# A message-passing kernel: 60 instead of 52 row-wise tiles, another split of their rows between two queues, earlier first loads, and one result write per group

## The chip, the cores and the metric

The kernel runs on one core of one Trainium2 chip. The time is device microseconds of one execution; what is given for the kernel before is the median of 3 runs, 1981.78 us (1979.75 to 1982.48). The profile was taken of a further execution.

The engines are called TensorE (PE in the profile; PEld is its weight load), VectorE (DVE), ScalarE (ACT), GpSimd (POOL) and SyncE (SP). ScalarE and SyncE also issue DMAs; such an issue occupies the engine's queue of instructions and is shown as ACTq or SPq.

## The reference: what is computed

One layer of a graph network over 6250 nodes of 128 features and 206250 edges, which are sorted by their receiver. Cut to what matters:

```python
w = silu(edge_feats @ rad_W1 + rad_b1) @ rad_W2 + rad_b2      # 32 features an edge
w = w + silu(chi @ sph_W1 + sph_b1) @ sph_W2 + sph_b2         # 32 more
q = (x @ Wq)[receivers]; k = (x @ Wk)[senders]; v = (x @ Wv)[senders]
alpha = (q * w * k).reshape(-1, 8, 16).sum(-1) / 4 * cutoffs[:, None]
out = segment_sum(alpha[..., None] * v, receivers) / 16
x = layernorm(x + out)
```

## The kernel before, in words

**Tiling.** 128 edges are a tile, 4 tiles a quad (512 edges), 4 quads a group. There are 403 quads in 101 groups. The loop (lines 770 to 837) runs over groups and, in each, over four slots; each slot handles one quad in each of several stages, so a slot is the unit of time of the loop. `order` is the list of quads in the order of the slots.

**Before the loop** (lines 289 to 507) the table of k and v of all nodes, `kv_tab`, 1 KB a node, is computed and stored in DRAM. For the first 10 quads the x of the senders is gathered instead (`gather_x`, 40 indirect DMAs), and k and v are computed from it.

**Gathers.** For all later quads GpSimd issues one indirect DMA a tile (`gather`, line 134), which fetches 128 rows of `kv_tab` for 128 senders into `kv` (16 buffers). The gathers of a quad are issued 14 quads ahead, and each waits for a matmul of the slot in which it is issued, so that none runs ahead of TensorE by more than that.

**Row-wise tiles.** One tile in each of `ROW_TILES` = 52 quads is not gathered by GpSimd. Its 128 rows are fetched by 128 plain DMAs of 1 KB, issued one by one: 64 by SyncE and 64 by ScalarE (`load_rows`, line 173). The place of a row in the table is read from `at_i` into a register first; one instruction (line 186) fills the registers of up to `ROW_UNIT` = 32 rows, and it is emitted just ahead of the first of these rows. The 52 quads are spread evenly over slots 27 to 392 (`row_at`, line 141), and the rows of each are issued over the slots since the last such quad's rows, ending 8 slots before they are used: 7 or 8 slots for each, so about 9 rows a slot on each of the two queues. In the code order of a slot they come last (line 837), behind the slot's other work on ScalarE and SyncE.

**A slot's work, by engine.** TensorE: one matmul of the group's bookkeeping (lines 243, 252 or 655), the sums of the messages of the group before (line 614), the first layers of quad i+2 (line 516), the queries at the edges of quad i+1 (line 525) and the second layers of quad i+1 (`weigh`, lines 558 and 563). ScalarE: two silus for quad i+2 (line 546), which wait for TensorE's matmuls of that slot, a copy between them, in some slots a scaling of a result (line 693), and then the rows. VectorE: the product with k for quad i+1 (line 575, which waits for the gather), the scores and the messages of quad i (lines 583 to 602), one-hot tables and, for each group, the moments of the layer norm; every fourth group it also computes the inverse roots for four groups (lines 707 to 715). SyncE: x in slot 0 (`load_x`, line 281), edge features in slot 2 (`load_feats`, line 218), receivers in slot 3 (`load_rel`, line 229), finished results (`write_rows`, line 731) and the rows.

**Order.** All of it is written out by hand; every engine does its instructions in the order of the code.

The first loads: x and features of group 0 are issued while `kv_tab` is computed (lines 418 and 501); those of groups 1 and 2 only at the head of the loop (lines 757 to 762), where they stand behind the stores of `rel_lin` (line 506) and between the loads of `relb`.

Results: four groups become ready together, are scaled in four slots in a row, and each is written at least 3 slots later, at most one a slot, in whichever slot comes.

Of the kernel before, what the change touches and what calls it, by code (L numbers as in the profile page):

```python
# [21 lines left out]
SP = mybir.EngineType.SP  # L22
ACT = mybir.EngineType.Activation
# [22 lines left out]
ROW_BYTES = 2 * D * 4  # L46
XQ = 10
RING = 16
ROW_TILES = 52
ROW_FIRST = 20  # L50
ROW_LAST = 392
ROW_LEAD = 8
ROW_UNIT = 32
ROW_ACT = 64
XU = 4
WRITE_LAG = 3
READY_LAG = 2
# [3 lines left out]
XL = 3  # L61
# [6 lines left out]
def gnn_kernel(ctx, tc, x, src, dst, weight, edges, rad_W1, rad_b1, rad_W2, rad_b2,  # L68
# [104 lines left out]
    def load_rows(i):  # L173

        k = next((k for k in range(ROW_TILES) if i <= row_at[k] - ROW_LEAD), None)
        start = None if k is None else (row_at[k - 1] if k else ROW_FIRST) - ROW_LEAD + 1
        if k is None or i < start:
            return
        q = order[row_at[k]]
        slots = row_at[k] - ROW_LEAD + 1 - start  # L180
        table = kv_tab.bitcast(U8).rearrange("(o n) b -> o (n b)", o=1)

        def rows_by(engine, name, a, b):
            for e in range(a, b, ROW_UNIT):
                m = min(ROW_UNIT, b - e)
                rows = nc.values_load_multi_w_load_instructions(
                    at_i[k:k + 1, e:e + m], engines=(name,), min_val=0,
                    max_val=(N - 1) * ROW_BYTES,
                    skip_runtime_bounds_check_because="senders are nodes")[1]
                for p, r in zip(range(e, e + m), rows):  # L190
                    yield lambda p=p, r=r: signalled(engine.dma_start(
                        row_of[q][p:p + 1, 0, :].bitcast(U8), table[:, ds(r, ROW_BYTES)]))

        def signalled(o):
            tc.no_tile_sem_insts.add(o.ins.name)
            tc.add_to_no_dep_group(f"rows_{q}", o.ins)
            o.then_inc(row_sems[k % ROW_SEMS], 16)
            row_count[k % ROW_SEMS] += 16
            row_done[q] = row_sems[k % ROW_SEMS], row_count[k % ROW_SEMS]

        n = P - ROW_ACT
        if i == start:
            row_of[q] = quad_of("wide", 3, P)[:, :2, :].rearrange("p t d -> p (t d)")[:, None, :]
            rows_left[SP].append(rows_by(nc.sync, SP, 0, n))
            rows_left[ACT].append(rows_by(nc.scalar, ACT, n, P))
        for engine, m in ((SP, n), (ACT, ROW_ACT)):
            a, b = (math.ceil(m * j / slots) for j in (i - start, i - start + 1))
            next_rows(engine, b - a)
# [7 lines left out]
    def load_feats(g, mark=None):  # L216
        feats_of[g] = gp.tile([P, EG // 2], F32, name="feats", bufs=3)
        o = nc.sync.dma_start(feats_of[g], edges[g])
        if mark is not None:
            tc.add_manual_dep(o.ins, mark.ins.name, WAIT, reason="one signal of TensorE a quad")  # L220
# [51 lines left out]
    def load_x(g, mark=None):  # L272

        if g not in r_of:
            n = min(XU, NG - g)
            rows = nc.values_load_multi_w_load_instructions(
                gb_i[:1, g:g + n], engines=(SP,), min_val=0, max_val=(N - P) * D * 4,
                skip_runtime_bounds_check_because="the table is clamped to it")[1]
            r_of.update(zip(range(g, g + n), rows))
        x_of[g] = gp.tile([P, D], F32, name="x", bufs=XL + 4)  # L280
        o = nc.sync.dma_start(x_of[g].bitcast(U8), rows_from(x, r_of[g]))
        if mark is not None:
            tc.add_manual_dep(o.ins, mark.ins.name, WAIT, reason="one signal of TensorE a quad")
# [21 lines left out]
    with tc.tile_pool(name="nodes", bufs=1) as nodes, \  # L305
# [76 lines left out]

        rows_f = nodes.tile([P, ROW_TILES], F32, name="rows_f")

# [93 lines left out]
        for i, (k, n) in enumerate(work):  # L478
            if i + 2 < len(work):
                turn(*work[i + 2])  # L480
            kvs = k_and_v(k, n)
            for o, w in smalls[i:i + 1]:
                nc.scalar.dma_start(o, w)
            if i >= len(chunks):
                kv_of[k[0]] = kvs
                a = (i - len(chunks)) * 5 // 4
                for t in range(a * P + P, min(((i - len(chunks) + 1) * 5 // 4 + 1) * P, NT), P):
                    turn_rel(t)
                for f in beside.get(i, []):
                    f()  # L490
                continue
            store(k, kvs)
            if k + 8 < len(chunks):
                load_nodes(k + 8)
            if k == 4:
                nc.sync.dma_start(src_i, src)
            for f in beside.get(k, []):
                f()
            if i == len(chunks) - 1:
                load_rel(0, gp, 1)  # L500
                load_feats(0)
                nc.sync.dma_start(scale, weight)
        for q in order[XQ:AHEAD]:
            gathers(q)
# [5 lines left out]
    with tc.tile_pool(name="ps", bufs=1, space=PSUM) as pp, tc.tile_pool(name="loop", bufs=1) as lp:  # L510
# [243 lines left out]
            nc.vector.tensor_scalar(general, found, 0.0, None, op0=OP.is_gt)  # L754

        written, ready, ready_at = [], [], []
        load_feats(1)
        load_rel(1, lp, 4)
        load_feats(2)
        load_rel(2, lp, 4)  # L760
        for g in range(1, XL):
            load_x(g)
        silus(order[0], first_layers(order[0]))
        pick(1)
        q_at_edges(order[0])
# [4 lines left out]
        for g in range(NG - 1):  # L770
            for slot, j in enumerate((0, 2, 1, 3)):
                q = g * NQ + j
                i = g * NQ + slot
                turned, past, old = None, mark, marks
                if slot == 0 and g == CHECK + len(checks) + 1:
                    verdict()
                if slot == 0:
                    turned = turn_q(g + 1, pp.tile([P, EQ], F32, name="pq", bufs=2))
                if slot == 1 and 2 <= g:
                    turned = sum_group(g - 2)  # L780
                if slot == 2:
                    turned = make_q(g + 1, pp.tile([P, EQ], F32, name="pq", bufs=2))
                if 1 <= g:
                    for t in ((), (0, 1), (2,), (3,))[slot]:
                        mark = sum_quads(g - 1, t)
                first_layers(order[i + 2])
                mark = q_at_edges(order[i + 1])
                marks = weigh(order[i + 1])

                def copies():  # L790
                    if turned:
                        turned()
                    if 1 <= g and slot == 3:
                        part_sums(g - 1)

                silus(order[i + 2], mark, marks, copies)
                if ready and ready_at[-1] <= i:
                    scaled(*ready.pop(0), i)
                if i + AHEAD < len(order):
                    gathers(order[i + AHEAD], old[-QT:])  # L800
                multiply(order[i + 1], mark)
                messages(q, scores(q, marks=marks), marks=marks)
                if slot == 0:
                    if g + XL < NG:
                        load_x(g + XL, past)
                if slot == 2:
                    if g + 3 < NG:
                        load_feats(g + 3, past)
                if slot == 3 and g + 3 < NG:
                    load_rel(g + 3, lp, 4)  # L810
                if slot == 0 and 1 <= g:
                    one_hots(g)
                if slot == 1:
                    one_hots_T(g + 1)
                    if g + 2 < NG:
                        pick(g + 2)
                if slot == 2 and 1 <= g:
                    place(g - 1)
                write_rows(1, i)
                if slot == (3 if g < NG - 2 else 2):  # L820
                    if 2 <= g:
                        statistics(g - 2)
                if slot == 3:
                    if CHECK <= g < CHECK + len(checks):
                        checks[g - CHECK]()
                if g == NG - 3 and slot in (0, 2):
                    wide_one_hots(order[slot // 2 - 3])
                if g == NG - 2 and slot == 0:
                    wide_one_hots(order[-1])
                    n = nc.values_load(general, min_val=0, max_val=1)  # L830
                    place(g)
                    place(NG - 1)
                if g == NG - 3 and slot in (1, 3):
                    weigh_wide(order[slot // 2 - 3])
                if g == NG - 2 and slot == 1:
                    weigh_wide(order[-1])
                load_rows(i)
# [209 lines left out]
```

## Time and profile before

| | |
|---|---|
| median of 3 runs | 1981.78 us |
| the profiled execution | 1977.56 us |
| its span, first to last instruction | 1975.8 us |
| TensorE busy, share of the span | 90% |
| VectorE | 77% |
| GpSimd | 75% |
| ScalarE | 33% |
| gathers issued by GpSimd | 1520 of `kv_tab`, 40 of x |
| rows issued one by one | 3328 by SyncE, 3328 by ScalarE |
| granted TensorE clock, mean | 0.941 |

How to read it: the busy time of an engine leaves out register, semaphore and DMA-issuing instructions, so ScalarE's 33% and SyncE's absence from the list say nothing of how full their queues are. A group of the profile is a line, an engine, an operation and its tiles, with the count, the busy time in us and the mean of one in ns, and behind the bar the idle time of the engine just before, with what ended it.

### The profile page before, as it was taken

The numbers are of one execution on the slowest core, as the hardware profiler recorded it, in microseconds if no ns is written. First come the engines' busy times: TensorE is split into PE (matmuls) and PEld (weight loads), VectorE is DVE, ScalarE is ACT, GpSimd is POOL, SyncE is SP. The second block draws the span as 40 slices with busy tenths as digits, with TensorE's granted clock in tenths as the row PEclk, the third lists the DMA queues.
The fourth block names the chain that finished last, engine by engine and source line by source line (L and its number), as shares of the span: only waits on it lengthen the run. The fifth ranks groups of instructions, "written<-read, shape, count | busy, mean of one in ns | idle before, by whom it ended". The sixth has DMA issues, their size and how long they took to land. (4 is left out here: it accounts for less than half of the span.)

```text
span 1975.8 us, 57697 instructions
## 1 busy us (share of the span) xinstructions
PE 1781.9 (90%) x16014; PEld 1482.9 (75%) x16014; DVE 1520.3 (77%) x3403; ACT 642.5 (33%) x1362; POOL 1481.0 (75%) x1570
## 2 busy tenths in 40 slices
PE   9799999999998999998989889988988888888998
PEld 8687778777777777777877777777767777777776
DVE  6688788888877777777777777776877877777778
ACT  3233333333233333332323332323323333232334
POOL 7777777777777777777777777777777777777775
PEclk9899999999989989899989999899999999898989
DMA  9455555555555555555555555555545455555543
GB/s 318 144 153 155 158 154 157 149 148 151 159 155 156 149 159 152 147 155 145 157 144 156 155 147 154 149 150 149 157 142 158 143 156 155 145 154 147 155 142 94
DMA packets 152293, 304.92 MB, mean 154 GB/s; under 512 B 39852, under 2 KB 86300, under 8 KB 151964
## 3 DMA queue, kind: packets, MB, share of 16 engines
q0 software_dynamic: 74240, 201.95, 36.4%
q1 hardware_dynamic: 69568, 95.42, 15.1%
q10 hardware_dynamic: 8156, 3.82, 0.9%
q8 instruction: 127, 2.08, 0.4%
q14 instruction: 202, 1.65, 0.3%
HBM read 287.58 MB, written 13.46 MB: 152 GB/s over the span
## 5 line engine op out<-in xcount | busy, mean ns | idle before, releaser
L134 POOL DMA_INDIRECT kv<-kv_tab,src_i x1520 | 1440.9, 948 | 469.1 <-PE pw L563 174.0
L546 ACT ACTIVATE act<-ph,b 128x512 f32<-128x512 f32 x806 | 554.8, 689 | 1275.2 <-PE pq L525 767.4
L563 PE MATMUL pw<-w,act 128*128 128x128 f32 x6448 | 883.1, 294 | 0.0
L563 PEld LDWEIGHTS pw<-w,act 128*128 128x128 f32 x6448 | 803.6, 203 | 96.7 <-issue 79.8
L516 PE MATMUL ph<-feats,w 32*128 32x512 f32 x1612 | 521.8, 670 | 38.3 <-ACT act L546 35.7
L525 PE MATMUL pq<-q,hotT 32*128 32x128 f32 x3224 | 489.3, 293 | 19.1 <-DVE kq L575 18.8
L575 DVE TENSOR_TENSOR kq<-pq,kv 128x512 f32<-128x512 f32 (+1 forms) x403 | 270.6, 671 | 285.4 <-DMA kv<-kv_tab,src_i 123.5
L525 PEld LDWEIGHTS pq<-q,hotT 32*128 32x128 f32 x3224 | 409.9, 195 | 49.8 <-DVE kq L575 47.9
L585 DVE TENSOR_REDUCE side<-kq 128x32 f32<-128x512 f32 x403 | 279.8, 694 | 42.7 <-PE pw L563 1.3
L602 DVE TENSOR_TENSOR msg<-kv,side 128x512 f32<-128x512 f32 (+1 forms) x404 | 270.3, 669 | 44.2 <-DVE side L589 2.4
L583 DVE TENSOR_TENSOR kq<-pw,kq 128x512 f32<-128x512 f32 x403 | 274.0, 680 | 0.0
L516 PEld LDWEIGHTS ph<-feats,w 32*128 32x128 f32 x1612 | 143.3, 190 | 144.4 <-ACT act L546 74.1
L558 PE MATMUL pw<-brow,onesb 3*128 3x512 bf16 x403 | 158.9, 394 | 0.6 <-DVE kq L583 0.6
L614 PE MATMUL po<-msg,hot 128*32 128x128 f32 x3200 | 156.8, 294 | 0.0
L655 PE MATMUL pq<-part,to 128*128 128x128 f32 x200 | 48.7, 328 | 88.8 <-DVE kq L575 88.5
L589 DVE TENSOR_TENSOR side<-side,scale 128x32 f32<-128x32 f32 x400 | 79.8, 200 | 42.6 <-DVE side L585 0.9
L655 PEld LDWEIGHTS pq<-part,to 128*128 128x128 f32 x200 | 32.9, 207 | 100.3 <-DVE kq L575 86.7
L614 PEld LDWEIGHTS po<-msg,hot 128*32 128x32 f32 x3200 | 72.3, 112 | 38.9 <-issue 5.6
L258 DVE TENSOR_TENSOR hotT<-relb,side 128x512 f32<-128x512 bf16 x101 | 68.7, 680 | 0.0
L252 PE MATMUL pq<-wq,xT 128*128 128x128 f32 x200 | 44.3, 305 | 26.5 <-DVE kq L575 26.1
L263 DVE TENSOR_TENSOR hot<-rel,side 128x512 f32<-128x512 f32 x100 | 68.0, 680 | 0.0
L252 PEld LDWEIGHTS pq<-wq,xT 128*128 128x128 f32 x200 | 32.4, 203 | 32.1 <-DVE kq L575 31.4
(121 smaller groups left out, 843.7 us busy)
## 6 DMA issues: line engine op xcount, KB each, us to landing
wide<-kv_tab SPq DMA_DIRECT2D x3328, 1.0 KB
wide<-kv_tab ACTq DMA_DIRECT2D x3328, 1.0 KB
feats<-in_edges SPq DMA_DIRECT2D x101, 512.0 KB
kv<-kv_tab,src_i POOLq DMA_INDIRECT x1520
relb<-rel_lin SPq DMA_DIRECT2D x101, 128.0 KB
x<-in_x SPq DMA_DIRECT2D x101, 64.0 KB
out<-y SPq DMA_DIRECT2D x101, 64.0 KB
kv_tab<-kv SPq DMA_DIRECT2D x12, 512.0 KB
```

The lines of the kernel that those rows point to most:

```text
L134: return nc.gpsimd.indirect_dma_start(out=o, out_offset=None, in_=table, in_offset=bass.IndirectOffsetOnAxis(ap=index, axis=0))
L516: return nc.tensor.matmul(act_of[q, i], w1[r0:r0 + R, :], feats_of[g][r0:r0 + R, c0:c0 + EQ], start=True, stop=True)
L525: o = nc.tensor.matmul(pq_of[q][:, t, :], hotT_of[g][b, t * P:(t + 1) * P], q_of[g][b, :], start=True, stop=True)
L546: o = nc.scalar.activation(act, act_of[q, i], AF.Silu, bias=b1[:, i:i + 1])
L558: nc.tensor.matmul(pw, onesb, brow.rearrange("p t d -> p (t d)"), start=True, stop=False)
L563: o = nc.tensor.matmul(pw[:, t, :], act_of[q, i][:, t * P:(t + 1) * P], w2[:, i, :], start=False, stop=(t == QT - 1 and i == 1))
L575: o = nc.vector.tensor_tensor(kq_of[q][:, u, :], pq_of[q][:, u, :], kv[:, :, :D], op=OP.mult)
L583: nc.vector.tensor_tensor(m, pw_of[q][:, t, :], m, op=OP.mult)
L585: o = nc.vector.tensor_reduce(alpha, m.rearrange("p t (h e) -> p t h e", e=HD), AX.X, OP.add)
L602: o = nc.vector.tensor_tensor(msg_of[q][:, u, :].rearrange("p t (h e) -> p t h e", e=HD), kv[:, :, D:].rearrange("p t (h e) -> p t h e", e ...
L614: o = nc.tensor.matmul(po_of[g][j * W:(j + 1) * W, :], hot_of[g][:, j * QT + t, :], msg_of[g * NQ + j][:, t, :], start=(t == 0), stop=(t = ...
L655: nc.tensor.matmul(ph[:, :D], to[:n, 0, :], part[:n, :], start=True, stop=(g == 0))
```

## The change

- `ROW_TILES` goes from 52 to 60. The row-wise quads stand every 6 slots (48 times) or 7 slots (12 times) instead of every 7 or 8; eight gathers leave GpSimd.
- Of the 128 rows of each such tile ScalarE issues 68 and SyncE 60, instead of 64 each.
- The registers are filled 30 rows at a time on SyncE (two fills a tile, as before) and 23 at a time on ScalarE (23, 23 and 22: three fills a tile instead of two).
- x and features of groups 1 and 2 are issued right behind those of group 0, ahead of the load of `scale` and of the stores of `rel_lin`. The loads of `relb` stay where they were.
- A finished result is written only in slot 1 of a group, so one a group instead of up to one a slot.

```diff
-ROW_TILES = 52
+ROW_TILES = 60
 ROW_FIRST = 20
 ROW_LAST = 392
 ROW_LEAD = 8
-ROW_UNIT = 32
-ROW_ACT = 64
+ROW_ACT = 68
+ROW_UNITS = {SP: 30, ACT: 23}
...
         def rows_by(engine, name, a, b):
-            for e in range(a, b, ROW_UNIT):
-                m = min(ROW_UNIT, b - e)
+            for e in range(a, b, ROW_UNITS[name]):
+                m = min(ROW_UNITS[name], b - e)
...
                 load_rel(0, gp, 1)
                 load_feats(0)
+                for g in range(1, XL):
+                    load_x(g)
+                    load_feats(g)
                 nc.sync.dma_start(scale, weight)
...
         written, ready, ready_at = [], [], []
-        load_feats(1)
         load_rel(1, lp, 4)
-        load_feats(2)
         load_rel(2, lp, 4)
-        for g in range(1, XL):
-            load_x(g)
         silus(order[0], first_layers(order[0]))
...
                     place(g - 1)
-                write_rows(1, i)
+                if slot == 1:
+                    write_rows(1, i)
```

`XL` is 3, so the new loop covers groups 1 and 2.

## The prediction

> **What bounds the kernel now.** I read the page first, then GpSimd's part of the waits, then stretches of the run side by side, then ScalarE's timeline, since its queue is what the change loads.
>
> ```profile
> span 1975.8 us, 57697 instructions
> PE 1781.9 (90%) x16014; PEld 1482.9 (75%) x16014; DVE 1520.3 (77%) x3403; ACT 642.5 (33%) x1362; POOL 1481.0 (75%) x1570
> ...
> L134 POOL DMA_INDIRECT kv<-kv_tab,src_i x1520 | 1440.9, 948 | 469.1 <-PE pw L563 174.0
> ```
> ```profile
> POOL kv L134 <- PE pw L563: 174.0, 558, 3.9
> POOL kv L134 <- issue: 157.1, 513, 0.9
> DVE kq L575 <- DMA kv<-kv_tab,src_i: 123.5, 85, 3.5
> ```
> ```profile
> 1959.55 0.95 POOL L134 DMA_INDIRECT kv<-kv_tab,src_i  x1 [0.31 <-issue]
> 1960.80 0.95 POOL L134 DMA_INDIRECT kv<-kv_tab,src_i  x1 [0.30 <-PE pq L657]
> 1962.06 0.95 POOL L134 DMA_INDIRECT kv<-kv_tab,src_i  x1 [0.31 <-PE po L614]
> ```
>
> GpSimd's 75% is a full queue: a gather takes 0.95 us and 0.30 us pass to the next, whatever the releaser named (174.0 us over 558 times is 0.31 us each). The last gather ends at 1963.0 us, 12.8 us ahead of the end of the span. VectorE's largest wait for data is for a gather, 85 times.
>
> ```profile
> core 0: us, PE busy (x) PEld busy (x) DVE busy (x) ACT busy (x) POOL busy (x), PEclk, DMA share, GB/s
> 84.00:123.50 39.50, 39.50 (x398) 34.03 (x398) 35.47 (x68) 15.26 (x30) 29.87 (x32) 1.00 0.54 162
> 200.00:400.00 200.00, 187.66 (x1812) 157.16 (x1811) 165.58 (x361) 70.25 (x149) 150.79 (x160) 0.98 0.53 152
> 600.00:1800.00 1200.00, 1071.13 (x9643) 889.52 (x9641) 904.48 (x1997) 377.67 (x802) 907.80 (x958) 0.93 0.53 151
> ```
>
> These stretches show two regimes. TensorE has 16014 matmuls for 403 quads, 39.7 a quad. Ahead of the rows (84 to 123.5 us) it is busy throughout: 398 matmuls in 39.5 us, 3.94 us for 39.7. From 200 to 400 us, with rows, 1812 matmuls are 45.6 quads, 4.38 us each: compute is still working off the 14 quads that GpSimd is ahead, and is slower than TensorE alone. From 600 us on, 9643 matmuls are 243 quads, 4.94 us each, and 958 gathers in 1200 us are 1.253 us each: GpSimd sets the pace.
>
> **The change, part by part.**
>
> *Eight gathers fewer.* 8 x 1.253 = 10.0 us off GpSimd's queue. Eight more quads have two of VectorE's products split.
>
> ```profile
> 308.49 0.55 DVE L575 TENSOR_TENSOR kq<-pq,kv 128x384 f32<-128x384 f32 x1
> ...
> 308.96 0.28 DVE L575 TENSOR_TENSOR kq<-pq,wide 128x128 f32<-128x128 f32 x1
> ```
>
> Even if the smaller part were wholly added, that is 16 x 0.28 = 4.5 us, which VectorE (75% busy in the last stretch) hides; I put it at 0.
>
> *The first loads.*
>
> ```profile
> 55.93 2.92 DVE L388 TENSOR_SCALAR rows_f<-src_i 128x1 f32<-128x1 int32 x47
> ...
> 61.44 2.17 SPq L445 DMA_DIRECT2D rel_lin<-relT  x2
> ...
> 67.25 2.05 PE L563 MATMUL pw<-w,act 128*128 128x128 f32 x16
> ...
> 68.77 2.46 SPq L281 DMA_DIRECT2D x<-in_x  x3
> ...
> 76.41 0.77 PE L243 MATMUL pq<-pick,x 128*128 128x128 f32 x2 [7.11 <-DMA x<-in_x]
> ...
> 79.53 3.26 PE L563 MATMUL pw<-w,act 128*128 128x128 f32 x16
> ...
> 82.31 0.95 POOL L134 DMA_INDIRECT kv<-kv_tab,src_i  x1 [3.88 <-PE pw L563]
> ```
>
> TensorE waits 7.11 us for x of group 1, then runs a quad's second layers in 3.26 instead of 2.05 us. GpSimd, which may be 14 quads ahead and no more, waits 3.88 us for these matmuls, 3.6 us more than its usual 0.30. With x issued ahead of the store at 61.44 us instead of behind it both go: compute starts 7.1 + 1.2 = 8.3 us sooner, less eight small VectorE instructions at 2.92 / 47 = 0.06 us, say 7.8 us; GpSimd gains 3.6 us. SyncE's four added issues ahead of `scale` and that store I put at 0: until 61.44 us SyncE waits for ScalarE's copies anyway, and `scale` is first used just ahead of the loop, behind the k and v of ten quads, which hide it. Without that cover its 0.8 MB and the 1.1 MB now ahead of it would delay the loop by some us, of the 7.8 just won.
>
> Were GpSimd to stay the bound, the sum would be -10.0 - 3.6 = -13.6 us.
>
> *ScalarE's queue.* This is the part that decides.
>
> ```profile
> 163.84 0.69 ACT L546 ACTIVATE act<-ph,b 128x512 f32<-128x512 f32 x1 [5.13 <-PE pw L563]
> ...
> 164.66 2.13 ACTq L191 DMA_DIRECT2D wide<-kv_tab  x7
> 166.90 0.69 ACT L546 ACTIVATE act<-ph,b 128x512 f32<-128x512 f32 x1 [1.63 <-PE pw L563]
> ...
> 167.72 2.44 ACTq L191 DMA_DIRECT2D wide<-kv_tab  x7
> 170.26 0.69 ACT L546 ACTIVATE act<-ph,b 128x512 f32<-128x512 f32 x1 [1.93 <-PE pq L525]
> 170.72 0.23 ACTq L191 DMA_DIRECT2D wide<-kv_tab  x1
> ...
> 171.04 5.07 ACTq L191 DMA_DIRECT2D wide<-kv_tab  x8
> 176.21 0.69 ACT L546 ACTIVATE act<-ph,b 128x512 f32<-128x512 f32 x1 [4.51 <-PE pw L563]
> ```
> ```profile
> L191 ACTq DMA_DIRECT2D wide<-kv_tab x3328: 227/228/563, 131.4 to 1884.0; - x196
> ```
> ```profile
> L186 SPq TENSOR_LOAD <-at_i x104: 1866/2177/2488, 120.3 to 1862.8; - x104
> L186 ACTq TENSOR_LOAD <-at_i x104: 2130/2204/2500, 128.9 to 1869.6; - x104
> ```
> ```profile
> L276 SPq TENSOR_LOAD <-gb_i x26: 476/572/650, 24.4 to 1889.6; - x26
> ```
>
> A slot without a register fill lasts 3.06 us (163.84 to 166.90) and has 9 rows. Seven rows span 2.13 us, six pitches and one issue of 0.23, so a pitch is 0.317 us; the run of 2.44 us, with one slow issue, gives 0.368. The median issue of 228 ns is the shortest but 1 ns, so I take 0.320. Without its rows the slot is 3.06 - 9 x 0.317 = 0.21 us. The run of 5.07 us with a fill is longer by 5.07 - (7 x 0.317 + 0.23) = 2.62 us, of which the fill is 2.2. Filling 4 registers takes 0.572 us, 32 take 2.204, so one more costs 0.058 us. A fill of 23 was not run; it lies between these two, and by the line through them the 2.62 become 2.10 us.
>
> Before: 3328 x 0.320 + 104 x 2.62 + 372 slots x 0.21 = 1415 us, 81% of the 1752.6 us from the first row to the last. After: 60 x 68 = 4080 rows x 0.320 = 1306, 180 fills x 2.10 = 378, 372 x 0.21 = 78: 1762 us. GpSimd's pace with 7.8 us of an earlier start leaves 1752.6 - 13.6 + 7.8 = 1747 us. So ScalarE's queue is full before it waits for anyone. In a slot it holds back the silus, by them TensorE, by TensorE all else.
>
> ```profile
> L713 DVE TENSOR_TENSOR h<-rs x75: 159/162/208, 124.5 to 1941.9; 128x4 f32<-128x4 f32 x72, 128x1 f32<-128x1 f32 x3
> ```
> ```profile
> 193.76 0.49 PE L655 MATMUL pq<-part,to 128*128 128x128 f32 x2 [1.97 <-DVE kq L575]
> ...
> 197.18 3.78 PE L563 MATMUL pw<-w,act 128*128 128x128 f32 x16
> ```
>
> It does wait: 75 of these in threes are 25 computations of inverse roots on VectorE, and behind one TensorE stands still for 1.97 us, so the silus come late. A slot without a fill now lasts 11 x 0.32 + 0.21 = 3.73 us, so TensorE's usual 3.94 us costs little; I take 1 us of each of the 25 (none to 2 us): 25 us. The rows then last 1762 + 25 = 1787 us from 131.4 - 7.8 = 123.6 on, to 1910.6, which is 26.6 us later than 1884.0.
>
> *Behind the rows* GpSimd's pace falls away, because compute is late and the data is there.
>
> ```profile
> 1964.11 0.39 PE L558 MATMUL pw<-brow,onesb 3*128 3x512 bf16 x1
> ```
>
> Before, 91.8 us pass from the last row to the end; now some 16 quads at 4.1 us (3.94 and the extra work of the last groups) and the 11.7 us behind the last quad's bias matmul: 77.3 us, 14.5 us less. This gain is also the slack by which ScalarE may be late unpunished.
>
> *One write a group* only moves SyncE's issues, which fit (below): 0.
>
> Sum: +26.6 - 14.5 = +12.1 us on the profiled execution's 1977.56, 1989.7 us; that execution is 4.2 us below the median of 1981.78, so 1994 us.
>
> **A rule against a row.** A fill's price by registers is 0.058 us in the rows above. The Trainium skill, Runtime: NRT & Kernel Launch, section Instruction fetch mechanics, has a register load at about 200 ns a register. By that the 32 would take 6.4 us and the fills' 4080 registers 816 us instead of some 300; the estimate would be 2500 us. The row of 2204 ns contradicts it for loads from on-chip memory, so the row decides.
>
> **The rivals.**
>
> 1. *GpSimd stays the bound* (faster): ScalarE's rows, waits included, fit into 1747 + 14.5 = 1761 us; it decides below that, 26 us under my sum. For it: my waits are a guess, and at 0.317 the rows take 12 us less. Against: nothing then may wait. 1977.56 - 13.6 = 1964.0, as a median 1968. That the change nets nothing is the middle between this and the forecast.
>
> 2. *TensorE's clock falls more often.*
>
> ```profile
> PEclk9899999999989989899989999899999999898989
> ```
>
> The clock of 0.93 from 600 to 1800 us means half speed for 14% of the time, there behind idle time. A slot with a fill lasts 5.8 us against TensorE's 3.94, so some 2 us are idle, 180 times. If a fifth of these end in a halved quad whose 1.2 us nothing hides, that is 36 x 1.2 = 43 us: 2037. Against: in a slot with a fill there is room for it. The Trainium skill, TensorE: Matmul & The Clock Gate, section HAM oscillation, sees the danger in idle gaps above about 3.4 us; by that the 2 us here would cost nothing and this rival fell away, but here the gap of 1.97 us was followed by second layers of 3.78 us instead of 2.05, so the trace disagrees and I keep it.
>
> 3. *SyncE is late.*
>
> ```profile
> L229 SPq DMA_DIRECT2D relb<-rel_lin x101: 532/555/682, 37.6 to 1904.6; - x101
> ```
>
> With 3600 rows x 0.320 = 1152, 120 fills at 2.18 and as much around them as ScalarE's = 312, and 93 groups x 4 other issues of 0.56 us at most = 208, it needs 1672 of 1747 us, which fits. But a result's buffer is reused two slots after its last write is issued; a SyncE that is two slots late stops VectorE there. 23 times half a slot of 4.8 us: +55 on the forecast, 2049.
>
> **How the numbers follow.** ScalarE sets the end: 0.50 (of it 0.11 within 0.2% of before, about what a measurement tells from no change, 0.03 faster, 0.36 slower). GpSimd stays: 0.28 (0.27 faster, 0.01 same). Clock 0.14 and SyncE 0.08, both slower. Faster 0.30, same 0.12, slower 0.58. The range goes from GpSimd's case, with 2 us off, to a forecast with all 50 us of waits and 10 us of slower issues, 1966 to 2028; the likeliest alone is 1980 to 2015.
>
> **What would show it.** Right: no wait of 7.11 us for x and none of 3.88 us on GpSimd; ScalarE's slots back to back, 3.7 and 5.8 us, with next to no idle queue; GpSimd's last gather near 1949 us and the end more than 20 us behind it; VectorE's wait for gathers near none; last row of ScalarE near 1910. Wrong: VectorE waiting for gathers as before and the last row near 1871 (rival 1); a mean clock below 0.9 (2); VectorE's moments waiting for a write (3).

## The result and the profile after

The changed kernel takes 2522.67 us (median of 4 runs, 2516.73 to 2526.2), against 1981.07 us of the kernel before: a ratio of 1.2731 (95% interval 1.2704 to 1.2757). The prediction was 1994 us in a range of 1966 to 2028: the sign is right, the size is off by 529 us. The profiled execution took 2516.73 us, at a mean granted clock of 0.822 (before 0.941).

The head of the page of the changed kernel, two of its costliest groups, and its chain of work that ended last:

```profile
span 2514.9 us, 59935 instructions
PE 2063.8 (82%) x16014; PEld 1749.7 (70%) x16014; DVE 1527.4 (61%) x3427; ACT 643.5 (26%) x1362; POOL 1474.3 (59%) x1562
...
ACTq 36%; issue 25%; PE 24%; ACT 7%; DVE 5%; POOL 1%; DMA 1%; DVEq 0%
...
L134 POOL DMA_INDIRECT kv<-kv_tab,src_i x1512 | 1433.5, 948 | 964.4 <-PE pw L566 657.2
...
L549 ACT ACTIVATE act<-ph,b 128x512 f32<-128x512 f32 x806 | 554.7, 689 | 1809.9 <-issue 951.7
```

GpSimd has 8 gathers fewer and no longer a full queue: it is idle ahead of its gathers for 964.4 us, which were 469.1 before. The chain is led by ScalarE's queue (ACTq, 36%). Of the 1809.9 us that ScalarE is idle ahead of its silus, "issue" ends 951.7 us: there nothing that the profile shows held them but their own engine's instructions. The waits say the same (us in total, times, longest), and below them stands the same wait of before:

```profile
ACT act L549 <- issue: 951.7, 123, 8.7
DVE kq L578 <- PE pq L528: 796.1, 303, 6.8
POOL kv L134 <- PE pw L566: 657.2, 549, 6.2
PEld ph L519 <- ACT act L549: 528.2, 342, 5.5
...
DVE kq L578 <- DMA kv<-kv_tab,src_i: 7.3, 4, 2.5
```
```profile
ACT act L546 <- issue: 43.2, 13, 5.0
```

So TensorE waits for the silus, VectorE and GpSimd for TensorE, and data is no longer waited for (7.3 us; before 123.5). Two of the stretches that were shown of before:

```profile
core 0: us, PE busy (x) PEld busy (x) DVE busy (x) ACT busy (x) POOL busy (x), PEclk, DMA share, GB/s
200.00:400.00 200.00, 163.62 (x1286) 138.36 (x1285) 119.71 (x265) 49.48 (x105) 119.61 (x127) 0.82 0.41 122
600.00:1800.00 1200.00, 981.81 (x7497) 832.95 (x7499) 704.47 (x1564) 296.10 (x627) 700.82 (x740) 0.80 0.41 117
```

7497 matmuls in 1200 us are 188.8 quads of 39.7, 6.35 us each, where it was 4.94. The rate is nearly the same from 200 to 400 us (6.17 us): it is the rows' steady pace and not a jam that builds up. Where the 6.35 us go is seen in ScalarE's timeline (start, duration, work; behind it the idle time before):

```profile
205.53 0.69 ACT L549 ACTIVATE act<-ph,b 128x512 f32<-128x512 f32 x1 [5.20 <-PE pw L566]
...
206.36 2.96 ACTq L191 DMA_DIRECT2D wide<-kv_tab  x9
209.42 0.69 ACT L549 ACTIVATE act<-ph,b 128x512 f32<-128x512 f32 x1 [2.46 <-PE pw L566]
...
210.17 0.69 ACT L549 ACTIVATE act<-ph,b 128x512 f32<-128x512 f32 x1
214.77 3.64 ACTq L191 DMA_DIRECT2D wide<-kv_tab  x11
218.51 0.69 ACT L549 ACTIVATE act<-ph,b 128x512 f32<-128x512 f32 x1 [7.66 <-issue]
```

A slot without a fill lasts 3.89 us (205.53 to 209.42). The next one lasts 9.09 us (209.42 to 218.51), and its eleven rows begin only at 214.77. Ahead of them stands a register fill of 5.09 us, which starts at 209.6, right behind the first silu, and overlaps the copy and the second one. All fills of the changed kernel (duration min/median/max in ns, first and last start), and all of ScalarE's rows:

```profile
L186 ACTq TENSOR_LOAD <-at_i x180: 2066/5056/5440, 124.1 to 2419.2; - x180
L186 SPq TENSOR_LOAD <-at_i x120: 2088/4466/6947, 115.2 to 2402.2; - x120
```
```profile
L191 ACTq DMA_DIRECT2D wide<-kv_tab x4080: 227/228/727, 126.6 to 2432.7; - x195
```

The rows cost what they did (median 228 ns). The fills do not: fewer registers each, and a median of 5056 ns on ScalarE where 32 took 2204. Taking the 180 in their order, the three of a tile have means of 2.13, 5.24 and 5.03 us; SyncE's two have 2.40 and 6.53 us. The first fill of each starts at element 60 or 0 of the tile's line in `at_i`, that is at byte 240 or 0; the slow ones start at bytes 332, 424 and 120. 240 and 0 are multiples of 16, the other three are not.

### The profile page after: what moved, and what is told of

Same layout as the page of the kernel before. It is cut to its first block, busy times and chain, and to the rows that moved or that the text cites. A ratio compares the mean times of both kernels' runs of the same rounds, so it can differ in the third digit from the quotient of the medians.

```text
span 2514.9 us, 59935 instructions
## 1 busy us (share of the span) xinstructions
PE 2063.8 (82%) x16014; PEld 1749.7 (70%) x16014; DVE 1527.4 (61%) x3427; ACT 643.5 (26%) x1362; POOL 1474.3 (59%) x1562
## 3 DMA queue, kind: packets, MB, share of 16 engines
q14 instruction: 221, 1.81, 0.2%
## 4 chain that ended last, share of the span: by engine, by line
ACTq 36%; issue 25%; PE 24%; ACT 7%; DVE 5%; POOL 1%; DMA 1%; DVEq 0%
ACTq L191 29%; PE pw L566 9%; ACTq L186 7%; PE ph L519 7%; ACT act L549 6%; PE pq L528 5%; POOL msg L134 1%; PE pw L561 1%; DVE side L588 1%; DVE kq L578 1%; DVE kq L586 1%; PE po L617 1%; DVE msg L605 1%; ACT y L696 1%; DMA kv<-kv_tab,src_i 0%
## 5 line engine op out<-in xcount | busy, mean ns | idle before, releaser
L134 POOL DMA_INDIRECT kv<-kv_tab,src_i x1512 | 1433.5, 948 | 964.4 <-PE pw L566 657.2
L566 PE MATMUL pw<-w,act 128*128 128x128 f32 x6448 | 1049.1, 329 | 0.0
L519 PE MATMUL ph<-feats,w 32*128 32x512 f32 x1612 | 694.5, 767 | 424.8 <-ACT act L549 423.8
L566 PEld LDWEIGHTS pw<-w,act 128*128 128x128 f32 x6448 | 963.8, 237 | 106.3 <-issue 92.6
L549 ACT ACTIVATE act<-ph,b 128x512 f32<-128x512 f32 x806 | 554.7, 689 | 1809.9 <-issue 951.7
L519 PEld LDWEIGHTS ph<-feats,w 32*128 32x128 f32 x1612 | 212.2, 216 | 578.0 <-ACT act L549 528.2
L528 PE MATMUL pq<-q,hotT 32*128 32x128 f32 x3224 | 570.8, 327 | 1.9 <-DVE kq L578 1.9
L528 PEld LDWEIGHTS pq<-q,hotT 32*128 32x128 f32 x3224 | 481.8, 225 | 4.7 <-DVE kq L578 4.1
L561 PE MATMUL pw<-brow,onesb 3*128 3x512 bf16 x403 | 179.1, 444 | 0.6 <-DVE kq L586 0.6
L696 ACT ACTIVATE y<-y,shift,rs 128x128 f32<-128x128 f32 x100 | 49.8, 499 | 1.1 <-DVE shift L690 1.1
L134 POOL DMA_INDIRECT msg<-in_x,src_x x40 | 38.9, 974 | 13.3 <-issue 11.6
L347 PE MATMUL pk<-wkv,xT 128*128 128x256 f32 x178 | 44.1, 391 | 1.6 <-DVE kv L348 1.6
```

Of the source, the lines that this page charges most:

```text
L134: return nc.gpsimd.indirect_dma_start(out=o, out_offset=None, in_=table, in_offset=bass.IndirectOffsetOnAxis(ap=index, axis=0))
L519: return nc.tensor.matmul(act_of[q, i], w1[r0:r0 + R, :], feats_of[g][r0:r0 + R, c0:c0 + EQ], start=True, stop=True)
L528: o = nc.tensor.matmul(pq_of[q][:, t, :], hotT_of[g][b, t * P:(t + 1) * P], q_of[g][b, :], start=True, stop=True)
L549: o = nc.scalar.activation(act, act_of[q, i], AF.Silu, bias=b1[:, i:i + 1])
L561: nc.tensor.matmul(pw, onesb, brow.rearrange("p t d -> p (t d)"), start=True, stop=False)
L566: o = nc.tensor.matmul(pw[:, t, :], act_of[q, i][:, t * P:(t + 1) * P], w2[:, i, :], start=False, stop=(t == QT - 1 and i == 1))
```

## The experiments

The theory: a fill whose first place is not at a multiple of 16 bytes takes some 0.2 us a register, one at a multiple takes about a quarter of that, and this is most of the 542 us between 1981.07 and 2522.67. Its rival: the cost is that of more and smaller fills, more rows on ScalarE or 60 tiles as such, however the list lies. A second question came up on the way: what 60 tiles cost when the fills are cheap. Each ratio below is to the kernel before, run on the same chip; times of runs on different chips can differ by a few us for that reason alone (the kernel before takes 1973.94 to 1981.07 us on those used here).

**1. Fills of 24 and 32.** The changed kernel, ScalarE's rows in fills of 24, 24 and 20, SyncE's in 32 and 28, so that all start at multiples of 16 bytes.

```diff
-ROW_UNITS = {SP: 30, ACT: 23}
+ROW_UNITS = {SP: 32, ACT: 24}
```

> The changed kernel with register fills of 24 rows on ScalarE (columns 60, 84, 108 of the list of places) and 32 on SyncE (columns 0, 32) instead of 23 and 30; every fill then starts at a multiple of 16 bytes. Theory A (a fill that starts at a multiple of 16 bytes reads four registers at a time, about 0.23 us for each four and 0.21 us for each one left over; any other start costs about 0.21 us a register): ScalarE's fills take 1.7, 1.7 and 1.5 us instead of 2.1, 5.2 and 5.0, SyncE's 2.2 and 2.0 instead of 2.4 and 6.5. ScalarE's queue then needs 1306 + 180 x 2.0 + 78 = 1744 us for the rows, about what GpSimd leaves, and the time falls to 1965 to 1995 us. Rival R (the second and later fills of a tile are slow when they do not begin at register 32): the fills at 84 and 108 stay at 5 us, that at 32 is fast, time near 2400.

Measured: 2054.59 us, ratio 1.0397 (1.0377 to 1.0416).

```profile
L186 ACTq TENSOR_LOAD <-at_i x180: 1534/1702/2082, 119.8 to 1957.2; - x180
```
```profile
ACT act L549 <- PE pw L566: 723.5, 234, 5.7
...
ACT act L549 <- issue: 224.8, 53, 5.1
```

468 of the 542 us are gone (by the ratios, 23.3 of 27.3 percentage points) with one line that changes neither tiles nor rows. The wait on "issue" falls from 951.7 to 224.8 us. But 2054.59 is still above the 1965 to 1995 that I expected: something of 60 tiles remains.

**2. The same counts, another layout.** The changed kernel with its 23, 23, 22 and 30, 30, but the list stored with gaps, so that each fill starts at a multiple of 16 bytes (elements 0, 32, 64, 88 and 112). The list is wider by 16 elements, and five small copies make it instead of one.

```diff
+AT = {0: 0, 30: 32, 60: 64, 83: 88, 106: 112}
...
-                    at_i[k:k + 1, e:e + m], engines=(name,), min_val=0,
+                    at_i[k:k + 1, AT[e]:AT[e] + m], engines=(name,), min_val=0,
```

> The changed kernel with the same fills of 23, 23, 22 and 30, 30 registers, but the list of places stored with gaps, so that the five fills start at columns 0, 32, 64, 88 and 112 (multiples of 16 bytes); five small copies instead of one ahead of the loop. Theory A: ScalarE's fills 2.1, 2.1 and 1.9 us, SyncE's 2.4 and 2.4; ScalarE's queue needs 1306 + 442 + 78 = 1826 us, time about 2030 to 2060. Rival R (register numbers or the count decide): nothing moves, 5.2 and 5.0 us and 6.5 us, time near 2520.

Measured: 2099.12 us, ratio 1.0615 (1.0584 to 1.0646). Number and size of the fills are those of the changed kernel, and 424 of the 542 us are gone, so the rival falls. The time itself is above the 2030 to 2060 that I expected, as in run 1.

```profile
L187 ACTq TENSOR_LOAD <-at_i x180: 1869/2104/2301, 122.1 to 2009.8; - x180
```

A fill of 23 takes 2.1 us here, more than the 1.70 us of one of 24 in the run before it: the registers beyond a multiple of four cost extra.

**3 and 4. The kernel before, its list moved.** By two elements (8 bytes), and by four (16 bytes); nothing else. `2:2 + P` in the first, `4:4 + P` in the second.

```diff
-    at_i = const.tile([ROW_TILES, P], I32, name="at_i")
+    at_i = const.tile([ROW_TILES, P + 16], I32, name="at_i")[:, 2:2 + P]
```

> The kernel before with its list of places moved by 2 columns, 8 bytes; counts, registers and everything else as before. Theory A: all four fills of a tile take 0.34 + 32 x 0.21 = 7.1 us instead of 2.2; SyncE's queue then needs 1065 + 104 x 7.5 + 190 = 2035 us for the rows where 1752 were there, and the time goes to about 2250 us. Rival R: nothing changes, 1981.

> The kernel before with its list of places moved by 4 columns, 16 bytes. Theory A with a boundary of 16 bytes: fills stay at 2.2 us and the time at 1981 within 5 us. If the boundary is larger than 16 bytes: fills slow as in the run with 8 bytes, about 2250 us.

Measured: moved by 8 bytes 2566.45 us, ratio 1.2986 (1.2952 to 1.3019); by 16 bytes 1974.77 us, ratio 0.9992 (0.9965 to 1.0019). The fills of the first and of the second:

```profile
L186 SPq TENSOR_LOAD <-at_i x104: 6486/6934/7299, 121.6 to 2456.1; - x104
L186 ACTq TENSOR_LOAD <-at_i x104: 6975/7188/7653, 130.2 to 2462.6; - x104
```
```profile
L186 SPq TENSOR_LOAD <-at_i x104: 1872/2181/2483, 120.6 to 1858.9; - x104
L186 ACTq TENSOR_LOAD <-at_i x104: 2127/2212/2549, 129.2 to 1868.1; - x104
```

Eight bytes alone break the kernel before, to more than the change did; sixteen do nothing. With runs 1 and 2, which repair the changed kernel, the theory is shown from both sides. The expected total for the move by 8 bytes was too low. The price of the fill was foreseen; but in that run a slot with a fill lasts some 11.2 us, and for some 390 us of the rows' stretch (my sum of the gaps in its queue) ScalarE's queue waits for others as well, which I had not counted.

**5 and 6. The two small parts alone.** The kernel before with the early loads only, and with one write a group only.

> The kernel before with the earlier loads of x and features of groups 1 and 2 alone. The prediction's step: GpSimd's wait of 3.88 us at the 15th quad goes, 3.6 us less, about 1974 us on this chip. Rival: the features ahead of the scale load and behind the stores of the table slow the start, and nothing or a loss of up to 3 us results.

> The kernel before with one result written per group (in slot 1) alone. The prediction's step: 0, 1977 within 4 us. Rival 3 of the prediction: VectorE's moments wait for the write of a result whose buffer is reused two slots later; such waits appear in VectorE's list, and the time grows by 10 us or more.

Measured: early loads 1973.71 us, ratio 0.9988 (0.9979 to 0.9997); one write 1982.19 us, ratio 1.0024 (1.0013 to 1.0035). The loads gain the few us expected: GpSimd's last gather ends at 1958.3 instead of 1963.0 us, and GpSimd's gap of 3.88 us is not there. The write was expected to cost nothing and costs 0.24%: GpSimd's last gather ends 4.4 us later, by new gaps of 1.41, 1.93 and 2.03 us between 364 and 421 us. Which late instruction makes these gaps I did not find.

**7 and 8. Aligned fills, even split, fewer tiles.** The changed kernel with 64 rows on each queue in fills of 32, with 60 and with 56 tiles.

```diff
-ROW_ACT = 68
-ROW_UNITS = {SP: 30, ACT: 23}
+ROW_ACT = 64
+ROW_UNITS = {SP: 32, ACT: 32}
```

> The changed kernel with 64 rows on each queue and fills of 32, as the kernel before had them: 60 tiles, early loads and one write a group. Theory (ScalarE's queue sets the end when it needs more than GpSimd leaves): ScalarE needs 3840 x 0.32 + 120 x 2.62 + 372 x 0.3 = 1655 us where 1747 are there, so GpSimd keeps the pace on that side, 10.0 + 3.6 us off: 1964 us. But SyncE needs 3840 x 0.33 + 120 x 2.25 + about 200 = 1737 of 1747; if SyncE's queue binds in the same way, its rows come late, VectorE waits for them, and the time is 1980 or more.

> As the run with 60 tiles and 64 rows on each queue, with 56 tiles. Both queues have room (ScalarE 1544, SyncE about 1632 of some 1750 us), so GpSimd sets the pace: 4 x 1.253 + 3.6 = 8.6 us off, about 1969 us. If compute cannot keep up even here: no better than 1977.

Measured: 60 tiles 2061.9 us, ratio 1.0428 (1.0414 to 1.0441); 56 tiles 1998.95 us, ratio 1.0119 (1.0104 to 1.0135). Both are slower than their likelier expectation. With cheap fills, each four tiles more still cost time: 25 us from run 5 to run 8 (some 5 of them the one write a group, by run 6), then 63 us. In the run with 60 ScalarE's queue is not full: over 372 slots of the rows I add up gaps of 190 us in which it waits for others, against 48 in run 1. SyncE's nearly is: between 600 and 1600 us the gaps of over 0.15 us between its queue's records sum to 28 us in 1000; it was 118 before. So the next theory was S: 64 rows of 60 tiles fill SyncE's queue; its rival A: a slot of ScalarE with a fill of 32 lasts long (a median of 6.7 us) and leaves TensorE idle, whose clock drops (0.902).

**9 to 11. Which queue.** Run 9 is the kernel before with 60 tiles and nothing else. Run 10 is the changed kernel with 56 rows on ScalarE (fills of 28) and 72 on SyncE (fills of 24). Run 11 is run 7 with ScalarE's fills cut to 16. The edits of runs 10 and 11 are shown against run 7.

```diff
-ROW_TILES = 52
+ROW_TILES = 60
```
```diff
-ROW_ACT = 64
-ROW_UNITS = {SP: 32, ACT: 32}
+ROW_ACT = 56
+ROW_UNITS = {SP: 24, ACT: 28}
```
```diff
-ROW_UNITS = {SP: 32, ACT: 32}
+ROW_UNITS = {SP: 32, ACT: 16}
```

> The kernel before with 60 tiles of single rows and nothing else changed: 64 rows of each by ScalarE, fills of 32 that start at multiples of 16 bytes, late loads and two writes a group as before. Theory T (the number of tiles by itself costs the time that was left in the run of 60 tiles with 64 rows, 2061.9): 2050 to 2065, with the same gaps of GpSimd, some 100 us. Rival W (the single write or the early loads cost it): 1965 to 1985, gaps of GpSimd under 30 us.

> The changed kernel with 56 rows of each tile by ScalarE (two fills of 28) and 72 by SyncE (three fills of 24), all fills at multiples of 16 bytes. Theory S (SyncE's queue, occupied 97 to 99% in the run with 64 rows, is what binds there): SyncE's tile grows by 8 x 0.32 + 0.8 = 3.4 us, 60 times, so 2062 + 200 = 2260, and ScalarE's waits grow. Rival A (the length of ScalarE's slots binds, TensorE waits for the eviction): ScalarE's tile falls by 8 x 0.32 + 0.3 = 2.9 us, so below 2062, about 2030.

> The changed kernel with 64 rows of each tile by ScalarE in four fills of 16 instead of two of 32, SyncE as in the run of 60 tiles with 64 rows (2061.9). ScalarE's queue holds some 0.8 us more a tile, but its longest slot falls from about 6.4 to 5.4 us. Rival A (long slots leave TensorE idle): 2010 to 2045, and TensorE's granted clock goes up from 0.90. Theory S (SyncE's queue binds): unchanged within 10 us of 2062.

Measured: run 9 2091.78 us, ratio 1.0595 (1.0574 to 1.0616); run 10 2181.32 us, ratio 1.1048 (1.1026 to 1.107); run 11 2061.24 us, ratio 1.044 (1.0419 to 1.0461). Run 9 shows that 60 tiles alone, with the fills of before, lose 6%, more than theory T's 2050 to 2065. Run 11 refutes A: ScalarE's slots with a fill fell from 6.7 to 5.5 us (medians), and TensorE's clock went up, to 0.934, with the time unchanged.

Run 10 goes as S says, if not as far (120 us slower than run 7, not 200). With 8 rows more a tile on SyncE, ScalarE's queue waits some 510 us, and VectorE waits for a buffer of the result, which is 15.6 us in run 7 (first line) and 363.9 in run 10 (the others):

```profile
DVE y L675 <- DMA out<-y: 15.6, 3, 5.6
```
```profile
DVE y L675 <- DMA out<-y: 363.9, 22, 19.9
...
PE pq L528 <- DVE kq L578: 289.4, 28, 17.2
```

The write that frees the buffer stands in SyncE's queue behind rows; VectorE stops, and TensorE behind it. The first such wait shows it: VectorE stands for 15.03 us and goes on at 290.72 us, the write is issued only at 285.03 us, and until then SyncE issues rows, loads and a register fill back to back. SyncE's gaps between 600 and 1600 us are 15 us in 1000 in run 10. In run 9 they are 25, and there SyncE itself stands still for the results, as its waits show beside those of run 7, and VectorE waits for rows, which it is not seen to do in run 7:

```profile
SPq L731 <- DMA out<-y: 136.2, 58, 9.9
```
```profile
DVE kq L575 <- DMA wide<-kv_tab: 62.9, 14, 9.5
```
```profile
SPq L734 <- DMA out<-y: 16.0, 8, 3.8
```

So with 64 rows of 60 tiles on SyncE, one write a group and the early loads together are worth 30 us (run 9 against run 7), though the write costs 5 us where SyncE has room (run 6).

With 60 tiles one of the two queues is always full or nearly so: ScalarE's at 68 rows (run 1, 2054.59 us), SyncE's at 72 (run 10). That SyncE's is also what holds runs 7 and 11 is argued from how full it is, and not shown: its gaps are 28 us in 1000 in run 7 and 46 in run 11, the waits by which it acts in runs 9 and 10 are short or absent there, and the chain of run 7 has SPq at 0% and ACTq at 18%. What costs 25 us at 56 tiles I did not separate either.

**12. Fewer tiles.** The kernel before with the early loads and 48 tiles.

> The kernel before with the early loads (1973.7 by itself) and 48 instead of 52 tiles. If GpSimd sets the pace at 52 tiles, four gathers more cost 4 x 1.25 = 5 us: 1978.7. If the rows' slots already cost TensorE time at 52 tiles, it is at or below 1973: by the slope from 52 to 56 tiles (1973.7 to 1999, 6 us a tile) it could be as low as 1960, which GpSimd's gathers forbid, so not below 1970.

Measured: 1975.53 us, ratio 1.0009 (0.9999 to 1.0018). That is 0.21% or 4.2 us above the ratio of run 5, as GpSimd's four gathers more (4 x 1.25 us) should cost. So at 48 and 52 tiles GpSimd sets the pace (in gaps ahead of its gathers it loses 1 us in either run), at 56 it no longer does all the time (30 us), and 52 with the early loads (run 5) is the best that was run: 0.12% faster than the kernel before (0.03 to 0.21%).

## Why the prediction was right and wrong

**The step that failed** is the price of a fill, in the term "180 fills x 2.10" of *ScalarE's queue*. I put 23 registers "between these two", 4 registers at 0.572 and 32 at 2.204 us, on a line. The line was drawn through two fills that start at multiples of 16 bytes; two of three new ones do not. Without what lies around it (0.42 us) I had a fill at 1.68 us, 302 us in all. Measured, the fills take 60 x (2.13 + 5.24 + 5.03) = 744 us: 442 us more. (SyncE's fills were priced in the same way and took 536 us instead of 262, but its queue has more room here: its gaps between 600 and 1600 us are 158 us in 1000.) Nothing in the profile of before could give this price, since all its fills there were alike; but it gave no upper bound either, and I took 2.204 us for one, as if fewer registers could not cost more. Even among aligned fills that is doubtful: 23 take 2.14 us and 24 take 1.70.

**The rule that I set aside was right for these fills.** The Trainium skill, Runtime: NRT & Kernel Launch, section Instruction fetch mechanics, states about 200 ns a register, and the estimate by it was 2500 us. The runs agree for the fills off 16 bytes (7.19 us for 32 registers, 5.06 and 5.27 us for 22 and 23) and disagree for the others (2.2 us for 32). My row contradicted the rule for one form of the instruction; I took it as a contradiction for all, and gave the rule's case no chance. That 2500 came so near to 2522.67 is partly luck: for all 4080 registers 816 us were reckoned, and the fills took 744, since the first fill of each tile is cheap (2.13 us); the other terms of the sum, which were too small, made up for it.

**What was right.** ScalarE's queue sets the end, by holding back the silus and through them TensorE and all else; the "issue" waits and the chain point to it, and run 1, which only makes the fills cheaper, agrees with it: ScalarE's fills take 438 us less and the kernel 468 us less. No run made the fills of one queue alone cheaper; that it is ScalarE's that count rests on the room in the two queues. The sum can be redone with the measured terms. Queue without waits: 744 us of fills and 1487 us for rows, slots and what surrounds the fills, 2232 us (forecast 1762, of it 302 and 1460). Waits in the queue, by its gaps, some 80 us (forecast 25). The rows then last 2312 us (forecast 1787): of the 525 us 442 are fills, 55 waits, 27 the slots, whose rest is larger (a slot of eleven rows without a fill takes 3.86 us on average, not 3.73). From the first row to the last it is 126.6 to 2432.7, 2306 us. Behind the last row 82.2 us pass to the end (forecast 77.3).

**Run 1 shows the rest of the error.** With fills at 1.70 us, near the assumed 1.68, the forecast should have held at 1994, and 2054.59 came. The rows' slots again take 1492 us beside the fills (forecast 1460), the waits 48 us, and the end behind the last row 85 us. So the terms for slots, waits and tail were each too small, some 60 us in sum, more than the distance from the forecast to its upper end: with the right price of a fill the forecast would still have missed.

**The other steps.** *Eight gathers fewer*: 1512 gathers, but GpSimd loses 501 us in gaps ahead of them, so nothing of the 10.0 us arrives; the last one starts at 2450.77, not near 1949.

*The first loads*: no wait of 7.11 us for x and none of 3.88 us on GpSimd, as forecast. The start of compute:

```profile
60.57 0.27 PE L393 MATMUL pt<-ident,rows_f 128*60 128x128 f32 x1 [2.87 <-DVE rows_f L388]
...
70.51 3.21 PE L566 MATMUL pw<-w,act 128*128 128x128 f32 x16
...
73.51 0.63 PE L243 MATMUL pq<-pick,x 128*128 128x128 f32 x2
...
75.58 2.05 PE L566 MATMUL pw<-w,act 128*128 128x128 f32 x16
```

The second quad's second layers come at 75.58 instead of 79.53 us: 4.0 us sooner, not 7.8. The first quad's come at 70.51 instead of 67.25, behind a wait of 2.87 us for the places of the 60 tiles (2.05 before), and they last 3.21 instead of 2.05 us. The eight small instructions more, which I had counted at 0.06 us each, are not the reason. With 60 tiles and the late loads (run 9) that matmul comes at 58.95 us without a wait; with the early loads and 52 tiles (run 5) it comes late as well:

```profile
60.10 0.27 PE L393 MATMUL pt<-ident,rows_f 128*52 128x128 f32 x1 [2.49 <-DVE rows_f L388]
```

In the nine traces with the early loads that matmul starts at 59.3 to 62.5 us, in the five with the late ones at 58.2 to 59.0. So the early loads themselves delay what stands ahead of the loop, mostly by 1 to 2 us, and that I had put at 0. By which wait they do so is not shown.

*One write a group* at 0 was wrong in both directions: it costs 5 us alone, and together with the early loads it is worth 30 us with 60 tiles of 64 rows on each queue; which of the two does that was not separated.

**The rivals.** GpSimd staying the bound fell already by the rows' slots, and in run 1 even with cheap fills. The clock dropped to 0.822, below the 0.9 that I had named as the sign of the second rival. I read it as a consequence of the long slots: ScalarE's queue waits for others for only some 80 of the 2312 us, so a slower TensorE can have cost it no more than that, and run 1, with cheap fills, has 0.917. In run 11 the clock rose and the time did not fall. Late SyncE, given 0.08, is not what the changed kernel shows, where VectorE is not seen to wait for a write; it is what 60 tiles do in run 10, in the form that was named (VectorE stopped at a result's buffer).

## What to carry to other kernels

An instruction whose operand may start anywhere can have a price for each kind of start: before costing a new size by interpolation, look whether the known sizes share an alignment which the new one loses, and take the size that keeps it (24 for 23). When a rule and a row disagree, ask which form of the instruction each was measured on before giving one of them no chance. And a queue that fits by the sum of its instructions' durations (SyncE's 1737 of 1747 us with 64 rows of 60 tiles) is to be treated as full: 15% more single rows, fills unchanged, cost 6%.

## What the runs showed of the hardware

- Filling registers from on-chip memory, by the median of each position. Starts at multiples of 16 bytes: 16 registers 1.21 to 1.33 us, 20 1.58, 24 1.68 to 1.81, 28 1.95 to 1.96, 32 2.13 to 2.28, and 22 1.92, 23 2.14, 30 2.35 to 2.38. Other starts (8 or 12 bytes past one): 22 5.06, 23 5.27, 30 6.51, 32 6.93 to 7.19 us. From 16 to 32 aligned registers that is some 0.06 us a register where the count is a multiple of four; what is left over, and all registers of a fill with another start, cost some 0.2 us each.
- A start at a multiple of 16 bytes was enough in every run: byte 240 is enough (2.14 us), byte 400 too (1.95 us for 28).
- Register fills and row-wise DMA issues are in no engine's busy time: the fills alone take 744 us on ScalarE in the changed kernel, and its busy time is 643.5 us. Its page has ScalarE 26% busy in the run in which its queue sets the end; before it was 33%. The "issue" of its own silus in the waits is where the full queue is seen.
